# One order for VectorE's work in every iteration of a fused four-convolution kernel

## The chip, the cores and the metric

The kernel runs on one core of one Trainium2 chip. The metric is the device time of one execution, in microseconds (us). Before the change three runs gave 503.2, 502.8 and 504.18 us, median 503.2. The profiled execution, from which every duration below comes, took 501.05 us, and its span in the profile is 499.2 us.

Five engines matter: TensorE (PE in the profile; PEld is its weight load), VectorE (DVE), ScalarE (ACT), GpSimd (POOL) and SyncE (SP), which issues the transfers. Each works through its own queue in order[...].

## The reference

The input is `x` of 128 samples x 64 channels x 1024 positions and a style vector of 128 for each sample. Four convolution layers follow one another, and `x` is added to the result:

```python
def _layer(x, style, w, b, mw, mb, typ):
    s = style @ mw.T + mb
    weight = SCALE * w * s[:, None, :, None]
    demod = lax.rsqrt(jnp.sum(weight * weight, axis=(2, 3)) + EPS)
    weight = weight * demod[:, :, None, None]
    ...
    # same: conv of 3 taps; upsample: transposed conv by 2, then blur (1,3,3,1)
    # downsample: blur, then conv by 2
for i, typ in enumerate(('same', 'upsample', 'same', 'downsample')):
    out = _layer(out, style, weights[i], biases[i], mod_w[i], mod_b[i], typ)
return x + out
```

Everything in the chain is linear in `x` once a sample's style is known. The kernel therefore multiplies the four weight stacks of a sample into one kernel of nine taps (the chain), and convolves `x` once with it. The three positions at either end of a row, where the padding of the single layers matters, are computed apart (the "ends").

## The kernel before, in words

**Tiling.** Two samples make a pair; their 2 x 64 channels fill the 128 partitions. There are 64 pairs, `p` = 0 to 63. A matmul uses a 64 x 64 quarter of the array[...]. The main loop has 32 iterations, `q`, each with two pairs, `p` = 2q and p + 1. In its first half it finishes pair p, in its second pair p + 1.

**The convolution of one pair.** A row of `x` is split into three planes of 344 positions, and the nine taps into three groups of three; a short convolution identity then needs five products for each group of taps in place of nine. VectorE and GpSimd prepare five inputs, held in a tile `T`:

- G (`pre1`, L489 and L494): two VectorE operations on `X`. The load of a later pair's first plane is issued after it.
- T12 (`pre1`, L500 and L501): GpSimd makes two of the five inputs from G.
- T3 (`pre2a`, L512): VectorE, from `X`; the load of the later pair's other planes is issued after it.
- T04 (`pre2b`, L522): VectorE makes the last two from G.

TensorE does the products: `convA12` and `convA3` (products 1, 2 and 3) into a PSUM tile `psA`, and `convB` (products 0 and 4) into the bank pair `Y`. Between them lie sums:

- `m1`: ScalarE copies product 1 from PSUM (L567).
- `seed1`: VectorE makes u, v and y1 from `psA` and m1 (three operations, L573).
- `seed2`: VectorE writes two sums into `Y` (two operations, L573), onto which `convB` then accumulates. There is one `Y` for nearly all pairs, so `seed2` of a pair waits until ScalarE has read the outputs of the pair before out of it, and `convB` waits for `seed2`.
- `output` (L630): ScalarE scales and adds the constant, from `Y` and y1; `store` sends the result.

**The chain.** Two or three iterations ahead, TensorE multiplies the weights: `stage1`, `stage2`, `stage3` (L352, L383, L420), with ScalarE's scaled copies (`scale3`, L330) between them. `combine` (L450 to L463) is VectorE's last step: six groups of operations, written as H, that make the weights of products 1 to 3.

**Extras.** A table `EXTRA` hangs small pieces of work on halves of iterations, nearly all of it VectorE's: the second and third part of the modulation (iterations 1 to 7) and the ends (iterations 6 to 25). `(q, 0)` comes at the end of VectorE's work in the first half, `(q, 1)` in the second. `SLOTS` puts TensorE's small matmuls for these into the middle of `convB(p + 1)`.

**Order.** The schedule is manual: each engine runs its instructions in the order in which the program's lines emit them. TensorE's order in an iteration, with c = q + 2 and s = q + 3, is stage2(c), convB(p), stage3(c, 0), convA12(p + 2), stage3(c, 1), convA3(p + 2), convB(p + 1), stage1(s), convA12(p + 3), convA3(p + 3). The order of VectorE's work in an iteration before, for most q:

- first half: T3 and T04 of p + 3, G of p + 4, seed1 and seed2 of p + 1, EXTRA (q, 0);
- second half: T3 and T04 of p + 4, G of p + 5, seed1 and seed2 of p + 2, combine(c), EXTRA (q, 1).

Iterations 0, 1, 2 and 30 have orders of their own. Iteration 0 also holds the inverse, a Newton step and the table tA for the samples 16 to 31 (`var_inverse`, `var_newton`, `table_A` of `PART[1]`), ahead of T3(3).

**Start.** Before the first real matmuls, `zeros_to_y` multiplies zeros into `Y`; `blur_matmul` (L306) then builds the matrix `E` from the blur weights, and stage1(0), stage2(0) and so on fill the chain.

**End.** Pairs 60 and 62 use a bank pair of the chain's pool (`ps_w`, two tiles of one bank each), pair 61 uses `Y`, and pair 63 uses a tile of two banks from the pool of `psA`, which four matmuls of zeros touch first. A tile of two banks counts as one object when accesses are ordered.

Of the kernel before, what the change touches and what calls it, by code (L numbers as in the profile page):

```python
# [54 lines left out]
C = 64  # L55
# [8 lines left out]
def kernel(  # L64
# [99 lines left out]
    def zeros_to_y(sets, n, p=0):  # L164


        for i in range(sets):
            rows = HALF[i % 2]
            for cols in HALF:
                nc.tensor.matmul(  # L170
                    y_bank(p, i % 2)[cols, :n], Z[rows, :C], Z[rows, :n], start=True, stop=True
                )
# [51 lines left out]
    def var_inverse(bs, ls=slice(0, NL)):  # L224
        nc_v.reciprocal(dm[:, ls, bs], nw[:, ls, bs])
# [9 lines left out]
    def first_inverse(bs):  # L235

        nc_v.reciprocal(d2, nw[:, 2, bs])
        newton(var[:, 2, bs], d2, n2)
# [51 lines left out]
    def blur_matmul(ps):  # L290


        n = len(BLUR2)
        plan = [[], []]
        for b in range(n):
            for r, (lo, hi) in enumerate(((0, 5), (5, NT))):
                i, j = max(lo, b), min(hi, b + K)
                if i < j:
                    plan[r].append((b, i, j, lo))
        for k in range(max(map(len, plan))):  # L300
            for r, rows in enumerate(HALF):
                if k >= len(plan[r]):
                    continue
                b, i, j, lo = plan[r][k]
                for cols in HALF:
                    nc.tensor.matmul(  # L306
                        ps[r][cols, C * (i - lo) : C * (j - lo)],
                        idn[rows],
                        w1s[rows, min(b, n - 1 - b), i - b : j - b],
                        start=(k == 0),  # L310
                        stop=(k == len(plan[r]) - 1),
                        skip_group_check=True,
                    )
# [210 lines left out]
    def pre2(p):  # L524
        pre2a(p)
        pre2b(p)
# [25 lines left out]
    def convA12(p):  # L552
        if p >= NP:
            return
        ps = ps_conv.tile([P, 2, 512], F32, tag="u", name=f"psA{p}")
        m = [ps[:, :, i * NB : (i + 1) * NB] for i in range(3)]
        product(p, 1, [m[0][:, s] for s in range(2)])
        product(p, 2, [m[1][:, s] for s in range(2)])
        part[p] = m
# [37 lines left out]
    def seed(p):  # L597
        seed1(p)
        seed2(p)
# [22 lines left out]
    def output(p, s, eng=nc_a, parts=((0, 2), (2, 3))):  # L622

        b = 2 * p + s
        d3, add = dm[:, 3, b : b + 1], oc[:, b : b + 1]
        for i, j in parts:
            dst = os[p][:, s, i * NB : j * NB]
            src = y1s[p][:, s] if i == 2 else y_bank(p, s)[:, i * NB : j * NB]
            if eng is nc_a:
                nc_a.activation(dst, src, AF.Identity, bias=add, scale=d3)  # L630
            else:
                eng.tensor_scalar(dst, src, d3, add, op0=ALU.mult, op1=ALU.add)

    def store(p, s, at=slice(0, 3 * NB)):
        nc.sync.dma_start(out[p, :, s, at], os[p][:, s, at])
# [254 lines left out]
    LATER = slice(PART[0].stop, B)  # L890
    n_later = NL * (B - PART[0].stop)
    L2, L01, L3 = slice(2, 3), slice(0, 2), slice(3, 4)
    zeros_to_y(2, 256)
    zeros_to_y(2, 512)
    nc_v.tensor_scalar_mul(mbs, mb, SCALE)
    mod_matmul(PART[0], pm[0][0])

    nc_a.activation(wsq[T, L2], wio[T, L2], AF.Square)
    blur_scale((0, 1))
    zeros_to_y(2, 256)  # L900
    mod_scale(PART[0], pm[0][0])
    mod_square(PART[0])
    q2_sum(L2)
# [3 lines left out]
    nc_v.tensor_mul(wsq[T, L01], wio[T, L01], wio[T, L01])  # L907
    var_root(PART[0], pm[0][1], L2)
    blur_scale((2, 3))
    zeros_to_y(2, 192)  # L910
    nc_a.activation(wsq[T, L3], wio[T, L3], AF.Square)
    psB = [Y[:, r] for r in range(2)]
    blur_matmul(psB)
    first_inverse(PART[0])
    table_A(PART[0], d2)
    scale3(0, BOTH)
# [144 lines left out]
    for q in range(NQ):  # L1061
        p = 2 * q
        c, s = q + 2, q + 3
        if q == 1:
            nc.sync.dma_start(Xe, x_ends)
        if q == 5:
            zeros()
        if c < NQ:
            stage2(c)
        convB(p)  # L1070
        output(p, 0)

        if c < NQ:
            stage3(c, 0)
        output(p, 1, nc_a if q < NQ - 1 else nc_v)
        if q == NQ - 1:
            store(p, 0)
            store(p, 1)

            convB(p + 1)  # L1080
            for i in (2, 0, 1):
                for r, eng in enumerate(BOTH):
                    output(p + 1, r, eng, ((i, i + 1),))
                    if i != 2:
                        store(p + 1, r, slice(0, NB) if i == 0 else slice(NB, HO))
            break
        convA12(p + 2)
        if q:
            if q < 3:

                (seed2 if q == 1 else seed)(p + 1)
            if q < NQ - 2:
                pre2(p + 3)
            store(p, 0)
            pre1(p + 4)
            store(p, 1)
            if q > 2:
                seed(p + 1)
            if q == NQ - 2:
                pre2(p + 3)  # L1100
        else:
            store(p, 0)
            store(p, 1)
            seed2(p + 1)
            var_inverse(PART[1])
            var_newton(PART[1])
            table_A(PART[1], dm[:, 2, PART[1]])
            for of in (table_C, vector_c0, table_3, vector_Da):
                of(PART[1])
            pre2(p + 3)  # L1110
            pre1(p + 4)
        EXTRA.get((q, 0), lambda: None)()
        if c < NQ:
            stage3(c, 1)
        convA3(p + 2)
        if q == NQ - 2:
            convA12(p + 3)
        side = SLOTS.get(q)
        convB(p + 1, (lambda: slot(*side)) if side else None)
        output(p + 1, 0)  # L1120
        if q == NQ - 2:
            seed(p + 2)
            convA3(p + 3)

            Y2[p + 3] = unit(ps_conv, "Y3")
            zeros_to_y(2, 2 * NB, p + 3)
        output(p + 1, 1, nc_a if q < NQ - 2 else nc_v)
        if q == NQ - 2:
            seed_last(p + 3)
        if c == NQ - 1:  # L1130

            banks = unit(ps_w, "Y2")
            Y2[p + 2] = Y2[p + 4] = banks
            zeros_to_y(2, 2 * NB, p + 2)
        if q:
            pre2(p + 4)
            store(p + 1, 0)
            pre1(p + 5)
            store(p + 1, 1)
        if q < NQ - 2:  # L1140
            seed(p + 2)
        if s < NQ:
            stage1(s)
        if s + 1 < NQ:
            scale3(s + 1)
        if c < NQ:
                combine(c)
        if q == 0:
            store(p + 1, 0)
            store(p + 1, 1)  # L1150
            pre2(p + 4)
        EXTRA.get((q, 1), lambda: None)()
        if q < NQ - 2:
            convA12(p + 3)
            convA3(p + 3)
        if q == 0:
            seed1(p + 3)
            pre1(p + 5)


# [64 lines left out]
```

## Time and profile before

| | |
|---|---|
| median of the runs | 503.2 us |
| profiled execution | 501.05 us |
| its span | 499.2 us |
| ScalarE busy | 322.5 us (65%) |
| GpSimd busy | 133.7 us (27%) |
| transfers | 70.90 MB, 142 GB/s |

How the pieces cost, mean duration of one instruction: G 889 and 519 ns, T12 929 and 946 ns (GpSimd), T3 508 ns, T04 890 ns, u 503 ns, v 499 ns, y1 511 ns, one instruction of seed2 518 ns, the operations of H 550 to 566 ns with two of 278 ns between. Consecutive operations of VectorE overlap by some 0.08 us, so the time from one start to the next is a little less. A line of a timeline gives start, duration, engine, line, operation, output and inputs, shapes and count, and in brackets the idle time before it with what ended it.

### The profile page before, as it was taken

To read this page: it belongs to the slowest core of one execution; us is meant where nothing else is said; L and a number is where in the kernel's file an instruction comes from. 1 tells how busy PE (TensorE), PEld (TensorE's weight loads), DVE (VectorE), ACT (ScalarE), POOL (GpSimd) and SP (SyncE) were. 2 spreads that over 40 slices of the span, in tenths; PEclk is the share of its full clock that TensorE was granted. 3 is DMA by queue.
4 is the path that set the end of the run, shared out by engine and by line. 5 is a ranking of instruction groups with operands and counts; after the bars stand their busy time and mean duration, and the time that the engine had idled before them with its cause. 6 is when DMAs were issued, how large, how long until landed. Compare 5 with 4: busy or idle time off the path is not lost.

```text
span 499.2 us, 28320 instructions
## 1 busy us (share of the span) xinstructions
PE 487.2 (98%) x12616; PEld 474.9 (95%) x12616; DVE 444.0 (89%) x937; ACT 322.5 (65%) x788; POOL 133.7 (27%) x195
## 2 busy tenths in 40 slices
PE   7999999899999999999999999999999999999994
PEld 5899989899999999999999999999999999999994
DVE  4989999999999979987979998879999889888895
ACT  4546757567666667667667667657667666766643
POOL 2234315345222212212222122212212212221210
PEclk8999999999999999999999999999999999999998
DMA  8125535454444445353445444435355435443123
GB/s 260 46 61 170 178 116 169 144 171 140 147 146 149 145 137 164 126 164 122 144 145 161 127 157 153 144 124 163 125 146 165 141 123 189 148 141 130 69 106 127
DMA packets 37449, 70.90 MB, mean 142 GB/s; under 512 B 4176, under 2 KB 28752, under 8 KB 37328
## 3 DMA queue, kind: packets, MB, share of 16 engines
q1 hardware_dynamic: 37248, 68.85, 43.0%
q8 instruction: 99, 1.62, 1.4%
q10 hardware_dynamic: 80, 0.25, 0.1%
q14 instruction: 22, 0.18, 0.1%
HBM read 35.46 MB, written 33.62 MB: 138 GB/s over the span
## 4 chain that ended last, share of the span: by engine, by line
PE 85%; DVE 11%; issue 1%; ACT 1%; DMA 1%; SPq 0%; DVEq 0%
PE psA L540 29%; PE Y L540 19%; PE psR L383 15%; PE psW L420 13%; PE psS L352 6%; PE psE L780 2%; DVE T L522 2%; DVE G L489 2%; DVE Y L573 2%; DMA par_oi<-in_params_oi 1%; DVE G L494 1%; DVE u L573 1%; DVE T L512 1%; DVE v L573 1%; DVE H L458 0%
## 5 line engine op out<-in xcount | busy, mean ns | idle before, releaser
L540 PE MATMUL psA<-T,H 64*64 64x170 f32 x4608 | 207.9, 304 | 0.5 <-ACT R L330 0.3
L540 PEld LDWEIGHTS psA<-T,H 64*64 64x64 f32 x4608 | 190.8, 133 | 1.4 <-issue 0.8
L540 PE MATMUL Y<-T,Wf 64*64 64x170 f32 x3072 | 141.9, 304 | 3.1 <-DVE Y L573 2.8
L500 POOL TENSOR_TENSOR T<-G 128x342 f32<-128x342 f32 x62 | 57.6, 929 | 318.5 <-DVE G L494 189.7
L540 PEld LDWEIGHTS Y<-T,Wf 64*64 64x64 f32 x3072 | 128.8, 133 | 5.7 <-issue 2.3
L630 ACT ACTIVATE o<-Y,oc,dm 128x340 f32<-128x340 f32 (+1 forms) x126 | 79.8, 634 | 60.1 <-PE Y L540 59.4
L420 PE MATMUL psW<-R,par_oi 64*64 64x256 f32 (+3 forms) x1536 | 100.2, 349 | 0.0
L573 DVE SCALAR_TENSOR_TENSOR Y<-psA,u 128x340 f32<-128x340 f32 (+1 forms) x134 | 66.7, 502 | 35.2 <-ACT o L630 32.9
L383 PE MATMUL psR<-S,E 64*64 64x192 f32 (+1 forms) x2304 | 93.9, 299 | 0.4 <-ACT S L330 0.4
L330 ACT ACTIVATE Wf<-psW,t 128x256 f32<-128x256 f32 (+1 forms) x252 | 75.3, 381 | 23.3 <-PE psW L420 23.1
L420 PEld LDWEIGHTS psW<-R,par_oi 64*64 64x64 f32 x1536 | 86.2, 133 | 3.1
L383 PEld LDWEIGHTS psR<-S,E 64*64 64x64 f32 x2304 | 86.9, 133 | 0.6 <-ACT S L330 0.5
L330 ACT ACTIVATE R<-psR,tC 128x448 f32<-128x448 f32 x63 | 36.5, 630 | 56.0 <-PE psR L383 56.0
L630 ACT ACTIVATE o<-y,oc,dm 128x170 f32<-128x170 f32 x125 | 65.8, 526 | 0.4 <-DVE y L573 0.4
L501 POOL TENSOR_TENSOR T<-G 128x342 f32<-128x342 f32 x62 | 58.6, 946 | 0.0
L522 DVE TENSOR_TENSOR T<-G 128x684 f32<-128x684 f32 x64 | 57.0, 890 | 0.0
L489 DVE SCALAR_TENSOR_TENSOR G<-X 128x688 f32<-128x688 f32 x64 | 56.9, 889 | 0.0
L352 PE MATMUL psS<-wd,par_oi 64*64 64x192 f32 x768 | 46.1, 329 | 0.0
L352 PEld LDWEIGHTS psS<-wd,par_oi 64*64 64x64 f32 x768 | 38.4, 136 | 0.5 <-ACT raw L648 0.3
L567 ACT ACTIVATE m<-psA 128x340 f32<-128x340 f32 x64 | 29.2, 456 | 10.1 <-PE psA L540 4.9
L573 DVE SCALAR_TENSOR_TENSOR y<-psA,v 128x340 f32<-128x340 f32 x64 | 32.7, 511 | 2.2
L494 DVE SCALAR_TENSOR_TENSOR G<-X 128x342 f32<-128x342 f32 x64 | 33.2, 519 | 0.0
(132 smaller groups left out, 384.7 us busy)
## 6 DMA issues: line engine op xcount, KB each, us to landing
out<-o SPq DMA_DIRECT2D x126, 255.0 KB, 2.8
X<-in_x SPq DMA_DIRECT2D x60, 344.0 KB, 3.1
X<-in_x SPq DMA_DIRECT2D x60, 172.0 KB, 3.2
X<-in_x SPq DMA_DIRECT2D x4, 516.0 KB, 6.5
Xe<-in_x_ends SPq DMA_DIRECT2D x1, 512.0 KB, 3.6
par_oi<-in_params_oi SPq DMA_DIRECT2D x2, 208.0 KB, 4.8
out<-o SPq DMA_DIRECT2D x2, 170.0 KB, 2.5
par_io<-in_params_io ACTq DMA_DIRECT2D x1, 240.0 KB, 3.8
```

Of the source, the lines that this page charges most:

```text
L330: nc_a.activation(dst, src, AF.Copy, scale=f)
L352: nc.tensor.matmul(ps[r][cols, k * C : (k + K) * C], woi[rows, 2, k, :], src[rows, :], start=(k == 0), stop=(k == K - 1), skip_group_check ...
L383: nc.tensor.matmul(ps[r][cols, lo * C : (lo + m) * C], E[rows, e + 2, :], src[rows, a, :], start=(n == 0), stop=(n == 8), skip_group_check ...
L420: nc.tensor.matmul(ps[r][cols, (lo - t_lo) * C : (hi - t_lo) * C], woi[rows, 0, k, :], rt[c][rows, lo - k : hi - k, :], start=(k == order[0]),
L489: nc_v.scalar_tensor_tensor(g[:, PL:], X[:, : 2 * PL], 0.5, X[:, PL:], op0=ALU.mult, op1=ALU.subtract)
L494: nc_v.scalar_tensor_tensor(plane(g, 2), plane(X, 3), 0.5, plane(X, 2), op0=ALU.mult, op1=ALU.subtract)
L500: eng.tensor_add(t[:, 2, :NJ], plane(g, 2), plane(g, 1))
L501: eng.tensor_sub(t[:, 3, :NJ], plane(g, 2), plane(g, 1))
L522: nc_v.tensor_sub(t[:, 0:2, :NJ], both(a, PL), both(b, 1))
L540: nc.tensor.matmul(ps[s][cols], w, Ts[p][rows, SLOT[m], j : j + NB], start=(g == 0 and m not in (0, 4)), stop=(g == 2), skip_group_check=True,
L573: nc_v.scalar_tensor_tensor(out, x, f, y, op0=ALU.mult, op1=ALU.add)
L630: nc_a.activation(dst, src, AF.Identity, bias=add, scale=d3)
```

## The change

The two halves of all iterations get one order of VectorE's work: G; the sums from PSUM (seed1, seed2); H; then T3 and T04. In the first half: G(p + 4), seed1(p + 1), seed2(p + 1), T3 and T04 of p + 3, EXTRA. In the second half: G(p + 5), seed1(p + 2), combine(c), seed2(p + 2), T3 and T04 of p + 4, EXTRA. seed1(3) and G(5) of iteration 0 follow this too. The work on `PART[1]` goes from the first half of iteration 0 to the end of its second half, and scale3(4) therefore from iteration 0 to iteration 1, on ScalarE. Stores stand after G and after seed2, and the loads tied to G and T3 move with them.

At the end pairs 61 and 63 use the two bank tiles of the chain's pool, pairs 60 and 62 use `Y`, and the tile `Y3` and its zeros go. The last pair's outputs are written as one piece of 170 columns (y1) and one of 340, in place of three of 170.

At the start the zeros are cut differently, with four matmuls of zeros behind the blur matmuls, and one of the two lists in `blur_matmul` is reversed.

```diff
+        plan[1].reverse()
...
-    zeros_to_y(2, 256)
-    zeros_to_y(2, 512)
+    zeros_to_y(4, 256)
+    zeros_to_y(2, 128)
...
-    zeros_to_y(2, 256)
+    zeros_to_y(4, 192)
...
-    zeros_to_y(2, 192)
     nc_a.activation(wsq[T, L3], wio[T, L3], AF.Square)
     psB = [Y[:, r] for r in range(2)]
     blur_matmul(psB)
+
+    for rows, ps in zip(HALF, pm[1]):
+        for cols in HALF:
+            nc.tensor.matmul(ps[cols, :192], Z[rows, :C], Z[rows, :192], start=True, stop=True)
...
         output(p, 1, nc_a if q < NQ - 1 else nc_v)
+        if q == 1:
+            scale3(c + 1)
...
-            for i in (2, 0, 1):
+            for i, j in ((2, 3), (0, 2)):
                 for r, eng in enumerate(BOTH):
-                    output(p + 1, r, eng, ((i, i + 1),))
-                    if i != 2:
-                        store(p + 1, r, slice(0, NB) if i == 0 else slice(NB, HO))
+                    output(p + 1, r, eng, ((i, j),))
+                    store(p + 1, r, slice(i * NB, j * NB))
             break
         convA12(p + 2)
+
+        pre1(p + 4)
+        store(p, 0)
         if q:
-            if q < 3:
-
-                (seed2 if q == 1 else seed)(p + 1)
-            if q < NQ - 2:
-                pre2(p + 3)
-            store(p, 0)
-            pre1(p + 4)
-            store(p, 1)
-            if q > 2:
-                seed(p + 1)
-            if q == NQ - 2:
-                pre2(p + 3)
-        else:
-            store(p, 0)
-            store(p, 1)
-            seed2(p + 1)
-            var_inverse(PART[1])
-            var_newton(PART[1])
-            table_A(PART[1], dm[:, 2, PART[1]])
-            for of in (table_C, vector_c0, table_3, vector_Da):
-                of(PART[1])
-            pre2(p + 3)
-            pre1(p + 4)
+            seed1(p + 1)
+        seed2(p + 1)
+        store(p, 1)
+        pre2(p + 3)
         EXTRA.get((q, 0), lambda: None)()
...
-
-            Y2[p + 3] = unit(ps_conv, "Y3")
-            zeros_to_y(2, 2 * NB, p + 3)
...
-            Y2[p + 2] = Y2[p + 4] = banks
-            zeros_to_y(2, 2 * NB, p + 2)
-        if q:
-            pre2(p + 4)
+            Y2[p + 3] = Y2[p + 5] = banks
+            zeros_to_y(2, 2 * NB, p + 3)
+        if q < NQ - 2:
+            pre1(p + 5)
             store(p + 1, 0)
-            pre1(p + 5)
-            store(p + 1, 1)
-        if q < NQ - 2:
-            seed(p + 2)
+            seed1(p + 2)
+        else:
+            store(p + 1, 0)
         if s < NQ:
             stage1(s)
-        if s + 1 < NQ:
+
+        if q and s + 1 < NQ:
             scale3(s + 1)
         if c < NQ:
-                combine(c)
+            combine(c)
+        store(p + 1, 1)
+        if q < NQ - 2:
+            seed2(p + 2)
+        pre2(p + 4)
         if q == 0:
-            store(p + 1, 0)
-            store(p + 1, 1)
-            pre2(p + 4)
+            var_inverse(PART[1])
+            var_newton(PART[1])
+            table_A(PART[1], dm[:, 2, PART[1]])
+            for of in (table_C, vector_c0, table_3, vector_Da):
+                of(PART[1])
         EXTRA.get((q, 1), lambda: None)()
         if q < NQ - 2:
             convA12(p + 3)
             convA3(p + 3)
-        if q == 0:
-            seed1(p + 3)
-            pre1(p + 5)
```

## The prediction

> **What bounds the kernel now.** I read the page's busy shares first, then the list of waits, then the timelines of VectorE, TensorE, ScalarE and GpSimd over one iteration of the loop, and last the first 120 us and the last 10 us.
>
> ```profile
> PE 487.2 (98%) x12616; PEld 474.9 (95%) x12616; DVE 444.0 (89%) x937; ACT 322.5 (65%) x788; POOL 133.7 (27%) x195
> ```
>
> ```profile
> DVE Y L573 <- ACT o L630: 32.9, 34, 3.1
> ```
>
> TensorE is the bound: by the table of stretches it is busy without a gap from 150 to 475 us. An iteration (two pairs) takes it 14.40 us: the first convB of two neighbouring iterations starts at 351.22 and 365.61. So nothing on VectorE can make these iterations shorter; a new order there can only close the few gaps of the start (the idle before matmuls of convB: 0.53 us at 65.25, 1.72 at 89.30, 0.36 at 119.05) and of the end, or open gaps. The 32.9 us in which VectorE waits for ScalarE's output is therefore cover and not cost. The question is how late each VectorE result comes for the matmul that needs it.
>
> ```profile
> 351.22 0.30 PE L540 MATMUL Y<-T,Wf 64*64 64x170 f32 x1
> ...
> 365.61 0.30 PE L540 MATMUL Y<-T,Wf 64*64 64x170 f32 x1
> ```
>
> ```profile
> 355.60 0.65 ACT L630 ACTIVATE o<-Y,oc,dm 128x340 f32<-128x340 f32 x1
> ```
>
> ```profile
> 356.30 1.07 DVE L573 SCALAR_TENSOR_TENSOR Y<-psA,u 128x340 f32<-128x340 f32 x2
> 357.27 0.75 DVE L853 TENSOR_TENSOR Ue<-Ve 128x576 f32<-128x576 f32 x1
> 357.94 0.51 DVE L512 TENSOR_TENSOR T<-X 128x342 f32<-128x342 f32 x1
> 358.36 0.87 DVE L522 TENSOR_TENSOR T<-G 128x684 f32<-128x684 f32 x1
> 359.14 0.87 DVE L489 SCALAR_TENSOR_TENSOR G<-X 128x688 f32<-128x688 f32 x1
> 359.93 0.51 DVE L494 SCALAR_TENSOR_TENSOR G<-X 128x342 f32<-128x342 f32 x1
> ...
> 361.74 1.07 DVE L573 SCALAR_TENSOR_TENSOR Y<-psA,u 128x340 f32<-128x340 f32 x2
> 362.71 0.55 DVE L458 SCALAR_TENSOR_TENSOR H<-Wf 128x384 f32<-128x384 f32 x1
> ...
> 365.57 0.69 DVE L853 TENSOR_TENSOR Ve<-Ue 128x512 f32<-128x512 f32 x1
> ```
>
> The reader is to see two deadlines. Write S for the start of convB(p). seed2(p+1), at 356.30, can't start before ScalarE has read the bank (355.60 + 0.65 = 356.25), which is S + 5.07; call it A. seed2(p+2), at 361.74, ends at 362.81, while its matmul comes at 365.61: 2.8 us to spare, because combine (H, 2.86 us from 362.71 to 365.57) comes after it.
>
> Two smaller facts carry numbers below. The first matmul of convB waits for both instructions of seed2, not for the first alone: here they end at 64.13 + 1.06 = 65.19 and the matmul starts 0.06 later.
>
> ```profile
> 64.13 1.06 DVE L573 SCALAR_TENSOR_TENSOR Y<-psA,u 128x340 f32<-128x340 f32 x2
> ```
>
> ```profile
> 65.25 1.96 PE L540 MATMUL Y<-T,Wf 64*64 64x170 f32 x48 [0.53 <-DVE Y L573]
> ```
>
> And H, behind a GpSimd operation, takes 1.12 us in place of 0.55; the next operation starts 1.04 us after it, not 0.47, so 0.57 us was lost.
>
> ```profile
> 80.07 0.94 POOL L501 TENSOR_TENSOR T<-G 128x342 f32<-128x342 f32 x1
> ```
>
> ```profile
> 80.30 1.12 DVE L458 SCALAR_TENSOR_TENSOR H<-Wf 128x384 f32<-128x384 f32 x1
> 81.34 0.47 DVE L450 SCALAR_TENSOR_TENSOR Wf<-par_oi,t,Wf 128x64 f32<-128x64 f32 x2
> ```
>
> [...] G, T3, T04 and H (two SBUF inputs) are stretched beside GpSimd's T12 (T04 1.59 for 0.86 us at 56.17), while u, v, y1 and seed2 (one input in PSUM) keep 0.5 us. [...] The trace has 0.50 from 8 to 11 us.
>
> **The change part by part.** Of every operation the durations are those of before; only order and the two bank tiles change.
>
> *Second half of an iteration.* Before: T3 and T04 of p+4, G of p+5, seed1 and seed2 of p+2, combine. After: G, seed1, combine, seed2, then T3 and T04. From A the new queue is: seed2(p+1), T3 and T04 of p+3, the extra work E of this half iteration, G of p+5, seed1(p+2), combine, seed2(p+2). From the rows above: 356.30 to 361.74 less the extra 0.67 (357.27 to 357.94) is 4.77; combine 2.86; seed2 1.07; matmul 0.06. That is A + 8.76. To it comes a port wait: T12(p+5) starts 0.16 after G ends and lasts 1.80 (355.16 to 356.96 for one iteration of GpSimd), so it ends some 2.47 us after the second G starts; H is issued 1.81 us after that G, 0.66 before T12's end. At 80.30 the same overlap of 0.71 cost 0.57, so 0.52 here (bounds 0 and 0.66). S to S becomes 5.07 + 8.76 + 0.52 + E = 14.35 + E, against TensorE's 14.40. Without extras it just fits (0.05 to spare). With an extra, TensorE waits E - 0.05, and everything after shifts, as ScalarE's output hangs on convB.
>
> *The extras* of first halves, as spans from their first start to the next operation on VectorE's timeline: iteration 8 0.67, 10 1.05, 11 0.65, 15 and 16 1.35 each, 20 1.33, 21 0.67, 22 0.60, 23 0.53, 25 1.27: 9.47, less 10 x 0.05 = 9.0 us. Iteration 9's (0.61) is hidden, since the ends' matmuls lengthen that convB by 2.2 us. Extras of second halves stand behind seed2(p+2), with 5.07 - 3.6 = 1.5 us before the next A: hidden, except 0.3 of iteration 3's 1.76, which A's own slack takes.
>
> *Iterations 0 to 7.* G(4) moves ahead of seed2(1) (before: 40.30). [...] seed2(1) starts near 42.4 and convB(1) goes from 41.66 to 43.5. T3 and T04 of 3 then meet T12(4): done near 46.2; G(5), seed1(2), the port wait, combine and seed2(2) end at 53.2. convB(2) goes from 49.45 to 53.3. The inverse, Newton step and tA (2.0 us) move from before T3(3) to behind T04(4), so VectorE's sum of work is the same: convB(4) goes from 65.25 to 68.6, convB(6) from 80.48 to 83.8. There before loses time of its own (gaps above; spans between convA12 of 15.85, 15.43, 16.71 against 14.5 plus small matmuls), which after doesn't repeat in the same places: convB(8) 97.44 to 98.9. But iterations 3, 4, 6 and 7 have first-half extras of 0.66, 2.29, 1.36 and 0.60: convB(10) 112.09 to 115.6, convB(14) 141.80 to 145.9, convB(16) 156.37 to 160.9. Sum +4.5 (bounds +1 and +7[...]). scale3(4) on ACT (0.80) sits in iteration 1 behind output(2,1), under that lateness: nothing.
>
> *Start.* The zeros have 4864 columns before and after. Four of 192 now stand between blur and stage1, where TensorE has no gap (7.57 to 11.4): +0.2. If the clock no longer halves, up to -1.7 (3.4 us at 0.50); zeros between 5.8 and 6.4 go, so I take no gain. The reversed blur plan has the same matmuls, gated by par_oi at 7.57: nothing.
>
> *End.* Pair 63's banks become two tiles, so its last outputs needn't take turns:
>
> ```profile
> 494.05 0.45 DVE L632 TENSOR_SCALAR o<-Y,dm,oc 128x170 f32<-128x170 f32 x1 [0.56 <-ACT o L630]
> 494.54 0.49 ACT L630 ACTIVATE o<-Y,oc,dm 128x170 f32<-128x170 f32 x1 [0.52 <-DVE o L632]
> 495.07 0.46 DVE L632 TENSOR_SCALAR o<-Y,dm,oc 128x170 f32<-128x170 f32 x1 [0.56 <-ACT o L630]
> ```
>
> Both engines write 340 columns side by side from 493.5 to 494.2 in place of 495.53; the two stores still follow each other (0.35): -1.0. Zeros for Y3 (0.79) go, but convB(63) waits for the seed at 491.45 anyway. Stores and loads change places on SP; X is needed over 14 us after its load is issued: nothing.
>
> Sum: 4.5 + 9.0 + 0.2 - 1.0 = +12.7. The profiled execution took 501.05 (span 499.2), so 513.8; the runs' median, 503.2, lies 2.15 above it, so I forecast 515.9.
>
> **Rivals.**
> *No port wait at H.* T12 might be out of the way. Then each such iteration has 0.57 to spare: of the extras' 9.5 us 3.8 stays, the start loses some 2.5, and the end gives 0.8 net of the zeros: +5.5, 508.7. Against it: the identical pair of operations at 80.30.
> *Faster.* If convB's first product needed only the first seed2 instruction (0.5 us earlier) and H didn't wait, 1.1 us would be free in every iteration and nearly all extras hidden; G ahead of the sums would fill VectorE's waits, and before's own losses of iterations 1 to 6 (4.5 us) and 1.0 at the end would go, while 0.9 us of extras stayed (15, 16, 20 and 25): 498.6. It decides at E below 1.1. For it: VectorE is full from 50 to 100 us, partly with port waits that the new order avoids. Against it: 65.25, and the two other waits of TensorE on seed2, at 89.30 and 491.50, which start 0.14 and 0.05 us after the last seed instruction.
> *Not seen at all.* The losses and gains of the start cancel and the extras mostly hide: 503.
>
> **Numbers.** Main case 0.62 (own range 511 to 519), no port wait 0.15, faster 0.17, no change 0.06. A measurement can tell about 0.3% (1.5 us) from no change. Faster 0.17, same 0.06, slower 0.77. The range 504.5 to 519 holds the two slower cases: its low end is extras with all slack, its high end 0.1 more per iteration and +7 at the start.
>
> **What would show it.** Right: TensorE's idle before convB of even pairs, released by Y of VectorE, in iterations 8, 10, 11, 15, 16, 20 to 23 and 25, each about the extra's length; H near 1.1 us; 14.4 us in the others; outputs of pair 63 side by side. Wrong: no idle there, or seed2(p+2) ending over 1 us before its matmul.

## The result, and the profile after

In one session the changed kernel took 520.65 us (median of 6 runs, 518.83 to 522.52) where the kernel before took 502.76 us (6 runs, 501.28 to 504.18). The ratio is 1.0353 with a 95% interval of 1.0321 to 1.0385. The profiled execution took 520.9 us with a span of 519.1 us. The ratios below are of fast runs, so an execution of a1 that took 730.43 us at a mean granted clock of 0.659, where its others took 500 to 504, is left out of its ratio.

First the page's busy shares of the changed kernel, then three lines of its list of waits (engine, output and line, what it waited for, then us in total, times, longest), and last the line of the kernel before that belongs to the third.

```profile
PE 494.0 (95%) x12624; PEld 462.4 (89%) x12624; DVE 463.8 (89%) x934; ACT 321.4 (62%) x787; POOL 136.7 (26%) x195
```

```profile
DVE Y L574 <- ACT o L631: 29.1, 26, 2.9
PEld Y L541 <- DVE Y L574: 20.1, 21, 3.1
PE Y L541 <- DVE Y L574: 17.1, 18, 2.9
```

```profile
PE Y L540 <- DVE Y L573: 2.8, 3, 1.7
```

VectorE's share is 89% before and after, so the share tells nothing. The wait of TensorE does: before, it waited 2.8 us in 3 places for the seeds in `Y`; now it waits 17.1 us in 18 places, and the growth of the span is 19.9 us.

The second halves show the chain. This is the timeline of the changed kernel from iteration 27 to iteration 28, without extras, VectorE first, then GpSimd, then TensorE's two convB with what lies between left out.

```profile
460.94 1.07 DVE L574 SCALAR_TENSOR_TENSOR Y<-psA,u 128x340 f32<-128x340 f32 x2 [1.18 <-ACT o L631]
461.92 0.51 DVE L513 TENSOR_TENSOR T<-X 128x342 f32<-128x342 f32 x1
462.34 0.87 DVE L523 TENSOR_TENSOR T<-G 128x684 f32<-128x684 f32 x1
463.30 0.88 DVE L490 SCALAR_TENSOR_TENSOR G<-X 128x688 f32<-128x688 f32 x1
...
465.90 1.08 DVE L459 SCALAR_TENSOR_TENSOR H<-Wf 128x384 f32<-128x384 f32 x1
466.90 0.47 DVE L451 SCALAR_TENSOR_TENSOR Wf<-par_oi,t,Wf 128x64 f32<-128x64 f32 x2
...
469.29 1.07 DVE L574 SCALAR_TENSOR_TENSOR Y<-psA,u 128x340 f32<-128x340 f32 x2
```

```profile
464.77 0.92 POOL L501 TENSOR_TENSOR T<-G 128x342 f32<-128x342 f32 x1 [4.42 <-DVE G L495]
465.64 0.93 POOL L502 TENSOR_TENSOR T<-G 128x342 f32<-128x342 f32 x1
```

```profile
455.84 1.96 PE L541 MATMUL Y<-T,Wf 64*64 64x170 f32 x48
...
470.41 0.81 PE L541 MATMUL Y<-T,Wf 64*64 64x170 f32 x16
```

From S = 455.84 to the next S = 470.41 are 14.57 us, where TensorE's own work is 14.40. The last seed2 ends at 470.36, 0.05 before its matmul; before, it ended 2.8 us ahead. H takes 1.08 us in place of 0.55 and costs 0.53 from start to start, beside T12, which ends at 466.57; this delay shows as a longer instruction and not as a wait between two. It is what the prediction and the expectations call the port wait; over the 32 iterations this operation takes 0.95 us in the mean, against 0.57 before (one of 1.12 at 80.30, the others 0.55 to 0.56), and the traces give its length, not its cause. One thing was not in the prediction: G starts 0.96 us after T04 (462.34 to 463.30), where before it was 0.78 (358.36 to 359.14).

TensorE's timeline of the changed kernel, its waits at the end of iterations 15, 16 and 29:

```profile
286.82 1.96 PE L541 MATMUL Y<-T,Wf 64*64 64x170 f32 x48 [1.03 <-DVE Y L574]
302.58 1.96 PE L541 MATMUL Y<-T,Wf 64*64 64x170 f32 x48 [1.12 <-DVE Y L574]
...
499.64 1.70 PE L541 MATMUL Y<-T,Wf 64*64 64x170 f32 x20 [2.92 <-DVE Y L574]
```

Waiting is not all that TensorE loses. The granted clock, the share of full speed that the profile gives for TensorE, is 0.50 from 116.66 to 120.07 us and again from 498.95 to 502.37, each time at or just behind the end of one of its two longest waits (2.76 us until 115.55, 2.92 until 499.64). Two stretches of the changed kernel show the first; each line gives the stretch, its length, the busy time and count of PE, PEld, DVE, ACT and POOL, the granted clock, and the transfers.

```profile
113.25:116.66 3.41, 1.11 (x32) 1.11 (x36) 3.34 (x7) 0.72 (x2) 2.62 (x15) 1.00 0.01 2
116.66:120.07 3.41, 3.41 (x44) 2.44 (x40) 2.68 (x6) 1.05 (x2) 1.77 (x3) 0.50 0.58 155
```

At half clock the 48 matmuls of convB(60) take 3.27 us, where convB takes 1.96 at full clock.

Where the time went is read by laying the first matmul of each pair's convB beside its place in the kernel before, both counted from convB(0). The sum of the terms is the difference of the spans.

| stretch | predicted | profiled executions |
|---|---|---|
| start, to convB(0) | +0.2 | +0.35 |
| iterations 0 to 7, to pair 16 | +4.5 | +6.30 |
| iterations 8 to 28, to pair 58 | +9.0 | +10.58 |
| end | -1.0 | +2.66 (+3.25 to pair 63, -0.59 behind it) |
| sum | +12.7 | +19.9 |

These are single executions, and the first row is less than starts differ from execution to execution: the changed kernel reaches convB(0) at 35.41 us, six kernels below with the same start at 34.76 to 36.93.

### The profile page after: what moved, and what is told of

It is laid out like the page before. It is cut to its first block, busy times and chain, and to the rows that moved or that the text cites. A ratio compares the mean times of both kernels' runs of the same rounds, so it can differ in the third digit from the quotient of the medians.

```text
span 519.1 us, 28314 instructions
## 1 busy us (share of the span) xinstructions
PE 494.0 (95%) x12624; PEld 462.4 (89%) x12624; DVE 463.8 (89%) x934; ACT 321.4 (62%) x787; POOL 136.7 (26%) x195
## 3 DMA queue, kind: packets, MB, share of 16 engines
q8 instruction: 99, 1.62, 1.4%
## 5 line engine op out<-in xcount | busy, mean ns | idle before, releaser
L541 PE MATMUL psA<-T,H 64*64 64x170 f32 x4608 | 188.0, 304 | 0.3 <-ACT R L331 0.3
L541 PEld LDWEIGHTS psA<-T,H 64*64 64x64 f32 x4608 | 171.2, 133 | 1.3 <-ACT R L331 0.5
L541 PE MATMUL Y<-T,Wf 64*64 64x170 f32 x3072 | 129.8, 309 | 17.2 <-DVE Y L574 17.1
L541 PEld LDWEIGHTS Y<-T,Wf 64*64 64x64 f32 x3072 | 113.0, 134 | 27.0 <-DVE Y L574 20.1
L631 ACT ACTIVATE o<-Y,oc,dm 128x340 f32<-128x340 f32 x125 | 79.5, 636 | 76.2 <-PE Y L541 74.1
L421 PE MATMUL psW<-R,par_oi 64*64 64x256 f32 (+3 forms) x1536 | 87.9, 353 | 0.0
L421 PEld LDWEIGHTS psW<-R,par_oi 64*64 64x64 f32 x1536 | 64.0, 134 | 13.5 <-issue 0.9
L353 PE MATMUL psS<-wd,par_oi 64*64 64x192 f32 x768 | 40.0, 324 | 0.0
L574 DVE SCALAR_TENSOR_TENSOR u<-psA,m 128x340 f32<-128x340 f32 x64 | 32.4, 506 | 3.3 <-ACT m L568 3.3
L353 PEld LDWEIGHTS psS<-wd,par_oi 64*64 64x64 f32 x768 | 32.4, 134 | 1.0 <-ACT raw L649 0.3
```

What stands on the lines that cost most here:

```text
L353: nc.tensor.matmul(ps[r][cols, k * C : (k + K) * C], woi[rows, 2, k, :], src[rows, :], start=(k == 0), stop=(k == K - 1), skip_group_check ...
L421: nc.tensor.matmul(ps[r][cols, (lo - t_lo) * C : (hi - t_lo) * C], woi[rows, 0, k, :], rt[c][rows, lo - k : hi - k, :], start=(k == order[0]),
L541: nc.tensor.matmul(ps[s][cols], w, Ts[p][rows, SLOT[m], j : j + NB], start=(g == 0 and m not in (0, 4)), stop=(g == 2), skip_group_check=True,
L574: nc_v.scalar_tensor_tensor(out, x, f, y, op0=ALU.mult, op1=ALU.add)
```

## The experiments

The theory on trial: seed2(p + 2) behind combine closes a chain through ScalarE's outputs, seed2, T3 and T04, extras, G, the sums, H with its delay beside T12, and seed2 again, and its length, not TensorE's work, now sets each iteration. The chief rival: VectorE simply has too much to do in a row, whatever the order of seed2 and combine. In the diffs the new order is that of the kernel named.

### a1: seed2 ahead of combine

```diff
+        if q < NQ - 2:
+            seed2(p + 2)
         if c < NQ:
             combine(c)
         store(p + 1, 1)
-        if q < NQ - 2:
-            seed2(p + 2)
```

> The changed kernel with one move back: in every second half seed2(p+2) stands before combine again, as before the change. Theory (the chain from ScalarE's last read of the bank to seed2(p+2) is what ends late): the chain loses combine and the port wait (2.86 + 0.52 us), so TensorE's idle before convB of even pairs vanishes in iterations 8 to 25 (9.5 us) and before pair 60 (2.9 us); what stays is at most the start, so 501 to 506 us. Rival (VectorE's sum of work, or its port waits, bound the iterations, and the order within one doesn't matter): 518 to 522, with the idle moved elsewhere.

Measured: 501.2 us, ratio to the kernel before 1.0008 (0.9995 to 1.0021). With two steps exchanged the whole loss is gone; the same VectorE work is done, so the rival falls for the loop. The timeline of a1 in iteration 28, VectorE and then TensorE:

```profile
462.81 1.08 DVE L574 SCALAR_TENSOR_TENSOR Y<-psA,u 128x340 f32<-128x340 f32 x2 [0.20 <-ACT o L631]
463.79 0.55 DVE L459 SCALAR_TENSOR_TENSOR H<-Wf 128x384 f32<-128x384 f32 x1
```

```profile
466.70 0.30 PE L541 MATMUL Y<-T,Wf 64*64 64x170 f32 x1
```

seed2 ends at 463.89, 2.8 us ahead of its matmul, and H, now behind T12, takes 0.55. Every iteration from 8 to 28 is back, within 0.05 us, at the length it has before. Three things stay. Pair 1 comes 1.07 us later than before (G(4) ahead of seed2(1), as e1 below shows). Pair 3 comes 2.90 later, which e1 does not cure; by pair 7 a1 is 0.67 earlier than before. And pair 61 loses 1.8 us to a wait taken up below.

### a2: extras in the time in which VectorE waits

```diff
         if q:
             seed1(p + 1)
+        EXTRA.get((q, 0), lambda: None)()
         seed2(p + 1)
         store(p + 1, 1)
         pre2(p + 3)
-        EXTRA.get((q, 0), lambda: None)()
```

> The changed kernel with the extras of the first halves put between seed1(p+1) and seed2(p+1), where VectorE waits about 1.2 us for ScalarE. Theory: extras up to about 1 us leave the chain, the long ones (1.35 us) leave 0.2 to 0.7 us each; TensorE's idle of iterations 8 to 25 falls from about 9.5 to 3 us, that of iterations 3 to 7 by 2 to 3 us; the rest stays: 509 to 513 us, and iterations without extras stay at 14.52 to 14.58 us. Rival (sum of VectorE's work): no change, 518 to 522.

Measured: 517.3 us, ratio 1.0328 (1.0302 to 1.0354): missed. The extras do leave the chain in part: iteration 20 falls from 15.69 to 14.60 us, but 21 only from 15.06 to 14.98 and 16 from 15.76 to 15.35. The timeline of a2, GpSimd and VectorE in iteration 16, tells why:

```profile
288.99 0.92 POOL L502 TENSOR_TENSOR T<-G 128x342 f32<-128x342 f32 x1
```

```profile
289.26 1.27 DVE L827 SCALAR_TENSOR_TENSOR Ue<-b1s,Ue 128x576 f32<-128x576 f32 x1
290.56 0.56 DVE L832 SCALAR_TENSOR_TENSOR Ue<-b1s,Ue 64x64 f32<-64x64 f32 x2
291.15 1.07 DVE L574 SCALAR_TENSOR_TENSOR Y<-psA,u 128x340 f32<-128x340 f32 x2
```

The wait before seed2 is just the time in which T12 runs. The extra meets it at 289.26 and takes 1.27 us, where it takes 0.75 in the changed kernel, and seed2 starts without any wait left, late. The expectation had counted the empty time and not the delay beside T12. Part of the miss lies elsewhere: iteration 4 became longer (18.82 us in place of 17.40), and after its wait of 2.51 us TensorE has half clock from 107.72 to 111.14.

### a3: T12 of second halves on VectorE, out of H's way

```diff
+        t12 = None
         if q < NQ - 2:
-            pre1(p + 5)
+            if p + 5 < NP:
+                g01, g2, t12 = pre1(p + 5, None)
+                g01()
+                g2()
...
         pre2(p + 4)
+        if t12:
+            t12(nc_v)
```

> The changed kernel with T12 of the second halves made by VectorE behind T04(p+4), so that no GpSimd operation stands beside H. VectorE gets 0.85 us more work in each iteration, behind seed2(p+2). Theory with the port wait as priced (0.52 us of the chain): H's first operation falls from 1.07 to 0.55 us, iterations without extras go to 14.39, those with extras lose 0.5 us of their idle each (14 of them, with those of iterations 3 to 7), and 0.5 before pair 60: 6 to 9 us less, 512 to 515. If the port wait is no part of the chain: no change or slower, 520 to 527, since the work grows by 27 us in all.

Measured: 512.93 us, ratio 1.0238 (1.0203 to 1.0273), as expected. VectorE has 0.85 us more to do in an iteration and the kernel is faster than the changed one by 1%: H's delay beside T12 lies in the chain, the sum of the work does not. The timeline of a3, VectorE from iteration 27 to 28:

```profile
457.97 0.55 DVE L459 SCALAR_TENSOR_TENSOR H<-Wf 128x384 f32<-128x384 f32 x1
...
463.00 0.51 DVE L501 TENSOR_TENSOR T<-G 128x342 f32<-128x342 f32 x1
463.43 0.51 DVE L502 TENSOR_TENSOR T<-G 128x342 f32<-128x342 f32 x1
463.85 0.87 DVE L490 SCALAR_TENSOR_TENSOR G<-X 128x688 f32<-128x688 f32 x1
...
467.46 1.08 DVE L574 SCALAR_TENSOR_TENSOR Y<-psA,u 128x340 f32<-128x340 f32 x2 [0.93 <-ACT o L631]
```

H is at 0.55 and VectorE waits 0.93 us for ScalarE afterwards: T12 fits into slack. Iterations without extras last 14.39 to 14.44 us, those with extras about 0.5 less than in the changed kernel.

### a4: seed2 ahead of combine in iteration 29 alone

```diff
+        if q == NQ - 3:
+            seed2(p + 2)
         if c < NQ:
             combine(c)
         store(p + 1, 1)
-        if q < NQ - 2:
+        if q < NQ - 3:
             seed2(p + 2)
```

> The changed kernel with seed2 before combine in iteration 29 alone (for pair 60). Theory: TensorE has only some 11.5 us of work in that iteration since the chain's stages have ended, and the 2.92 us of idle before convB(60) are the same chain: they go, 517 to 518.5 us. Rival (the new bank tiles of pairs 61 and 63 lengthen the end by themselves): at most 0.5 us less.

Measured: 517.48 us, ratio 1.0339 (1.0321 to 1.0356). By the traces pair 60 follows pair 58 after 11.54 us in place of 14.65 (11.49 in the kernel before), and the span falls from 519.1 to 516.4, by 2.7 us. The end is thus one more link of the same chain. a4 has no half clock at the end, and then waits 1.80 us for `psA`, a wait that the changed kernel does not have: of the 3.11 us won at pair 60, 2.43 are left at pair 63.

### b1: a third tile for G

```diff
-    gpool = ctx.enter_context(tc.tile_pool(name="gpool", bufs=2))
+    gpool = ctx.enter_context(tc.tile_pool(name="gpool", bufs=3))
```

> The changed kernel with a third buffer for the tiles G. In the changed order the first operation of G(p+5) overwrites the tile that T04(p+3), just ahead of it, reads, and it starts 0.96 us after T04 where 0.78 was usual. Theory: with a third buffer these 0.17 us leave the chain in second halves without an extra, so iterations 13, 17, 18 and 26 to 28 fall from 14.52 to 14.58 to 14.39 us; with an extra in between nothing changes: 1 to 1.5 us less than the changed kernel, 517 to 520. Rival[...]: no change of the 0.96.

Measured: 518.6 us, ratio 1.0335 (1.0312 to 1.0357); its interval overlaps that of the changed kernel, so the trace must tell. The timeline of b1, VectorE:

```profile
461.37 0.87 DVE L523 TENSOR_TENSOR T<-G 128x684 f32<-128x684 f32 x1
462.15 0.87 DVE L490 SCALAR_TENSOR_TENSOR G<-X 128x688 f32<-128x688 f32 x1
```

G again starts 0.78 us after T04. With two tiles, G of p + 5 overwrites the G of p + 3 that T04 just ahead of it reads, and the next instruction starts only when T04 is done. The program orders the two itself: T04 raises a semaphore of VectorE in 44 of its 64 cases in the changed kernel, in 1 in b1 and in the kernel before, and VectorE waits for this semaphore 318 times in the changed kernel, 275 times in b1. Iterations 13, 17, 18 and 26 to 28, which have no extra, fall from 14.52 to 14.71 us to 14.39 to 14.48; those with an extra, which stands between T04 and G, stay as they are. b2 below agrees: there T04 and G use different tiles, and the same six iterations last 14.39 to 14.48 us. Pair 58 comes 2.8 us earlier than in the changed kernel, 1.9 of it already at pair 16. Of that, 1.7 has nothing to do with the tile: it is the half clock of the changed kernel from 116.66 to 120.07 us, which b1's execution doesn't have. Both wait 2.76 us before convB(10). The changed kernel's timeline of the weight loads shows stops there:

```profile
118.50 0.26 PEld L421 LDWEIGHTS psW<-R,par_oi 64*64 64x64 f32 x4 [0.27 <-issue]
119.03 0.26 PEld L421 LDWEIGHTS psW<-R,par_oi 64*64 64x64 f32 x4 [0.27 <-issue]
```

"issue" means that the engine waited for nothing that the profile shows as an event; the clock is shown in another view. Why b1 keeps its clock is taken up in the last section.

### b2: the kernel before, with seed2 behind combine

```diff
         if q < NQ - 2:
-            seed(p + 2)
+            seed1(p + 2)
...
                 combine(c)
+        if q < NQ - 2:
+            seed2(p + 2)
```

> The kernel before with one part of the change alone: in second halves seed2(p+2) goes behind combine. Theory: the same chain, 14.35 us plus the extra, since G, seed1, H with its wait for T12 and seed2 follow A in the same way: about 9 us in iterations 8 to 25, about 3 before pair 60, 1 to 4 in iterations 3 to 7: 12 to 16 us above before, about the whole loss of the change. Rival (several parts of the change make the loss together): under 8 us above before.

Measured: 530.54 us, ratio 1.0593 (1.0556 to 1.063), twice the loss expected. The expected part is there: from pair 16 to 58 it loses 9.67 us (expected: about 9), and the iterations with extras are as long as in the changed kernel within 0.02 us. The unexpected part is the start: pair 16 comes 15.03 us late, against 6.30 in the changed kernel. TensorE's timeline of b2 has the waits:

```profile
52.26 1.96 PE L540 MATMUL Y<-T,Wf 64*64 64x170 f32 x48 [1.86 <-DVE Y L573]
70.47 3.37 PE L540 MATMUL Y<-T,Wf 64*64 64x170 f32 x48 [3.48 <-DVE Y L573]
90.93 3.38 PE L540 MATMUL Y<-T,Wf 64*64 64x170 f32 x48 [3.64 <-DVE Y L573]
```

In the second and third line the same 48 matmuls take 3.37 and 3.38 us in place of 1.96, since b2 has half clock from 69.99, 90.47 and 124.60 us, each time for 3.41 us and at the end of a wait of 2.77 to 3.64. The changed kernel has one such stretch in these iterations. So the rest of the change (G and the sums first, T3 and T04 last, the work on `PART[1]` later) gives back 8.7 us of what its one bad step costs in the first iterations; by an estimate from 3.41 us at 0.50, up to 3.4 of these are two stretches at half clock that it avoids. Which of the three parts gives it was not separated.

### b3: the kernel before, with the end's tiles and outputs alone

```diff
-            for i in (2, 0, 1):
+            for i, j in ((2, 3), (0, 2)):
...
-            Y2[p + 3] = unit(ps_conv, "Y3")
-            zeros_to_y(2, 2 * NB, p + 3)
...
-            Y2[p + 2] = Y2[p + 4] = banks
+            Y2[p + 3] = Y2[p + 5] = banks
```

> The kernel before with the change's end alone: pairs 61 and 63 in the chain's two bank tiles, 60 and 62 in Y, the last outputs in two pieces. Theory: the last outputs run side by side on ScalarE and VectorE, 0.5 to 1.0 us less than before; pair 60 isn't late, as seed2(60) stands ahead of combine. Rival (the bank tiles lengthen the end): 1 to 3 us more.

Measured: 500.65 us, ratio 0.9978 (0.9959 to 0.9996), 1.1 us (0.2 to 2.1). Its profile puts 0.27 us behind pair 63 (7.47 us from there to the end in place of 7.74). Of its other 0.9 us nearly all lies where the edit can have no part: 0.51 before convB(0), and 0.34 by pair 7. So that the outputs alone give 1.1 us is not shown. In the changed kernel itself the two outputs do stand side by side:

```profile
513.95 0.63 ACT L631 ACTIVATE o<-Y,oc,dm 128x340 f32<-128x340 f32 x1 [0.37 <-PE Y L541]
514.11 0.63 DVE L633 TENSOR_SCALAR o<-Y,dm,oc 128x340 f32<-128x340 f32 x1
```

### Toward a faster version: e1, f1, f2 and f3

e1 is a1 with three repairs: seed2(1) ahead of G(4) in iteration 0, T04(62) behind the sums of pair 61, and the third G tile.

```diff
+        if q == 0:
+            seed2(p + 1)
         pre1(p + 4)
...
+        if q == NQ - 2:
+            seed_last(p + 1)
+            pre2b(p + 2)
...
-        pre2(p + 4)
+        pre2a(p + 4)
+        if q != NQ - 3:
+            pre2b(p + 4)
```

> The kernel of the first experiment (seed2 ahead of combine) with three repairs: seed2(1) ahead of G(4) in iteration 0, seed2(61) ahead of y1(61) and T04(62) (TensorE waited 1.8 us there for psA), a third G tile. Theory: 1.0 us less at the start, up to 1.7 at the end: 1.5 to 3 us under the kernel before, 497.5 to 499.5 where before gives 500.7. If the start is bound by VectorE's sum of work: 0 to 1.5 us under before.

Measured: 502.28 us, ratio 1.0006 (0.9992 to 1.0021): missed. Pair 1 wins its 1.07 us, but at pair 3 nothing is left of it: e1 is 3.01 us later than before there, a1 2.90, since TensorE now waits 2.65 us at once before convB(3). The first repair moved the lateness from iteration 0 into iteration 1. And then it costs more: pair 4 comes 3.37 us late, in a1 1.62, because e1 has half clock just behind this wait.

```profile
61.26:64.67 3.41, 3.41 (x56) 3.41 (x52) 2.90 (x6) 0.98 (x3) 0.77 (x1) 0.50 0.59 160
```

The 22 executions of e1 form two groups, 8 from 499.52 to 500.80 us and 14 from 501.94 to 503.27; the profiled one (503.26) is of the second. That the others of that group lose their clock at the same place is likely and not shown. The second repair works: from pair 58 to 63 e1 takes 24.22 us, a1 24.82.

The f kernels go the other way: from b3, with the order of a1 only in a range of iterations.

```diff
+        new = 3 <= q < NQ - 3
+        if new:
+            pre1(p + 4)
+            store(p, 0)
+            seed(p + 1)
+            store(p, 1)
+            pre2(p + 3)
-        if q:
+        elif q:
...
+        if new:
+            pre1(p + 5)
+            store(p + 1, 0)
-        if q:
+        elif q:
...
+        if new:
+            store(p + 1, 1)
+            pre2(p + 4)
```

This is f3. In f1 the range begins at 2, in f2 at 3, and in both it ends with 29.

> The kernel before with pair 63's outputs side by side (as in b3), and in iterations 2 to 28 alone the changed order of VectorE's work, with the second seed2 ahead of combine; iterations 0, 1, 29 and 30 keep the order of before. Theory: what was good in the change is the order G, sums, then T3 and T04 in iterations 2 to 7 (a1 went from +1.61 us against before at pair 4 to -0.67 at pair 7), what was bad is seed2(1) behind G(4) in iteration 0, seed2 behind combine everywhere, and the end. Then convB(7) comes 2.2 us earlier than in the kernel before, that stays to the end, and with 0.5 to 1.0 for the outputs the time is 497.5 to 499 us where the kernel before takes 501, ratio 0.993 to 0.997. Rival: a1 only caught up from a late start, TensorE's work sets pair 7 in any case: then as b3, ratio 0.998, convB(7) 54.2 us after convB(0).

> As f1, but the changed order begins in iteration 3 and iteration 2 is that of the kernel before. Theory: the 1.72 us that TensorE waits before convB(7) in the kernel before come from T3(9), G(10) and the port in iteration 3 itself, so most of the 2.2 us is gained here too: 498 to 499.5 us, ratio 0.994 to 0.998. Rival: it is iteration 2's order that sets it (T3 and T04 of 7 ahead of G): then convB(7) stays 54.2 us after convB(0) and the ratio is that of b3, 0.998.

> As f2, but iteration 29 too keeps the order of the kernel before; the changed order, with seed2 ahead of combine, runs in iterations 3 to 28 alone. In f2 pair 58 came 1.37 us earlier than in the kernel before and pair 63 0.2 us earlier only: T3 and T04 of pair 62, last in iteration 29, push the sums of pair 61 behind them (482.65 in place of 481.30), and TensorE waits 1.78 us for the bank that they read. Theory: with T3 and T04 of 62 first again in iteration 29, pairs 60 to 63 come 23.7 us after pair 58 as in b3, and f2's gain stays: 1.4 us at pair 58 and 0.5 to 1.0 at the outputs, so 498.7 to 499.8 us where the kernel before takes 501.2, ratio 0.995 to 0.997. Rival: the wait before convA of pair 62 comes from another stage of the end that the changed order of iteration 28 also delays: then pair 63 stays where f2 has it, ratio 0.999.

| | median us | ratio, interval | pair 7 against before | pair 58 | pair 63 |
|---|---|---|---|---|---|
| f1 | 500.72 | 0.9989, 0.9976 to 1.0003 | -0.36 | -0.48 | +0.66 |
| f2 | 501.18 | 0.9991, 0.998 to 1.0002 | -1.54 | -1.37 | -0.21 |
| f3 | 499.99 | 0.996, 0.9945 to 0.9975 | -0.75 | -0.58 | -0.65 |

f1 and f2 missed their forecasts. f1's profiled execution has a stop of TensorE of 1.52 us that ends at 67.74 and that no releaser explains (the last section takes it up), and what it would be without that can't be read. f2's gain at pair 7 is there, and is lost at the end. A delay beside T12 in iteration 3, the port of its expectation, does not show: in the kernel before T3(9) takes 0.51 us there, and G(10), at 85.49, 0.87 and 0.51, as elsewhere. VectorE's and TensorE's timelines of f2:

```profile
480.98 0.55 DVE L463 SCALAR_TENSOR_TENSOR H<-Wf,H 128x384 f32<-128x384 f32 x1
481.44 0.51 DVE L512 TENSOR_TENSOR T<-X 128x342 f32<-128x342 f32 x1
481.87 0.86 DVE L522 TENSOR_TENSOR T<-G 128x684 f32<-128x684 f32 x1
482.65 0.51 DVE L573 SCALAR_TENSOR_TENSOR u<-psA,m 128x340 f32<-128x340 f32 x1
```

```profile
485.24 1.99 PE L540 MATMUL psA<-T,H 64*64 64x170 f32 x48 [1.78 <-DVE Y L573]
```

T3 and T04 of pair 62 stand between H and the sums of pair 61, and TensorE waits for the `psA` that these sums read. The changed kernel and a1 have the same order there; a1 has the same wait. f3 takes the old order in iteration 29, the wait is gone (pair 61 follows pair 59 after 12.14 us in place of 13.34), and the kernel is 0.4% faster than the kernel before. That is what f3's forecast said, but not by the way that it said: pair 58 comes 0.58 us earlier, not 1.4. Of its median gain of 1.5 us b3 as a whole already has about 1.1; that f3 beats b3 is not shown, the intervals overlap. In convB(4) its profiled execution has a stop of the weight loads without a releaser of 0.69 us, where f2's, at the same place, is 0.36.

## Why the prediction was right or wrong

**Right.** The direction, and the mechanism with its place and price. a1 shows that seed2 behind combine is the whole loss of iterations 8 to 28. The formula 14.35 + E was met where it was to hold: iteration 8 15.07 us (15.02 by the formula), 10 15.42 (15.40), 15 15.70 (15.70), 20 15.69 (15.68), 25 15.62 (15.62). Iteration 9 is hidden as said. H's delay beside T12 is 0.53 us (taken: 0.52), and a3 shows that it lies in the chain. Why VectorE's operation is longer there was not shown; what the traces have is 1.08 us in place of 0.55 for H and 1.27 in place of 0.75 for a2's extra. The outputs side by side go with 0.59 us less behind pair 63 (0.27 in b3).

**Wrong: the end.** The step "End: ... -1.0" priced only the bank tiles and outputs. The chain was worked out as 14.35 + E against TensorE's 14.40, and that comparison was carried to all iterations, but in iteration 29 TensorE has no stage of the chain left to do and needs 11.49 us. There the chain is not 0.05 us too short but 3.2 us too long (14.65). Pair 60 comes 3.16 us late. The end cost +2.66 in place of -1.0, the biggest miss of the sum (3.7 us). a4's span is 2.7 us shorter, 2.4 of it by pair 63. What is left in a4, 0.8 us at pair 63, fits T3 and T04 of pair 62 ahead of pair 61's sums, which f3 against f2 shows to be worth 1.2 us there. In the changed kernel itself TensorE, late and at half clock, does not wait for these sums; what the half clock of its end costs alone was not separated.

**Wrong in size: "Without extras it just fits (0.05 to spare)".** Six iterations (13, 17, 18 and 26 to 28) last 14.52 to 14.71 us in place of 14.39, together 1.2 us of the 1.6 between 9.0 and 10.58. The missing term is the G tile that T04 still reads, 0.18 us wherever no extra stands between the two: b1, without it, wins 0.93 us from pair 16 to 58, all in these six. The iterations with extras lose 9.38 in place of 9.0.

**Wrong in size: iterations 0 to 7, 4.5 against 6.30.** The steps to pair 10 were near and on the high side (pair 4 +2.42 for +3.35, pair 8 +0.58 for +1.5, pair 10 +3.32 for +3.5). The excess comes between pairs 10 and 11, from the half clock at 116.66: iteration 5 takes 16.24 us, in b1, without it, 14.51, and b1 has +4.42 at pair 16. The step that failed is the price of a wait: the prediction weighed the clock for the start alone, and took a wait of TensorE at its own length. Here the wait of 2.76 us cost 1.7 us more. Two of the changed kernel's six executions, with a mean clock of 0.997 in place of the profiled 0.990, took 518.83 and 518.85 us.

**Slips that changed nothing.** S + 5.07 is the start of seed2(p+1), at 356.30; ScalarE ends at S + 5.03. The places of convB(8), (10), (14) and (16) before are 97.22, 111.88, 141.53 and 156.10, 0.2 to 0.3 us ahead of those given; only differences entered the sum. The terms of the rival without a delay of H give some +5.2 us, not +5.5.

**The offset.** 2.15 us were added for the distance of the runs' median from the profiled execution. The changed kernel's profiled 520.9 lies at its median, so this addition covered part of the miss by luck: the sum was 7.2 us short, the forecast 4.75.

**The start, by luck.** No gain was taken from the clock at the start, and the +0.35 is near the +0.2 taken. But the half clock there comes and goes from execution to execution, as the last section shows, and moves convB(0) by more than that.

**The rivals.** H without a delay beside T12: out, by the 1.08 us. Faster, from a first seed2 instruction that frees the matmul: out, since the waits end 0.05 us after the second. Nothing seen: out.

## What to carry to other kernels

A chain that just fits under the bound in the steady loop is to be compared with the bound again in each iteration where the bound is shorter, the last ones first. A long wait of TensorE is to be priced above its length: in the loops of these profiles 12 of the 13 waits of 2.3 us or more went with 3.41 us at half clock, up to 1.7 us more each, and none of the waits up to 2.08 us did. Behind a3's wait of 2.33 us, until 490.85, the 48 matmuls of convB take 3.51 us; behind a2's of 2.08 us, until 53.78, they take 1.96. Before an operation is put into an engine's empty time, look at what runs on the neighbour engine in that very time: here it was T12, beside which H took 1.08 us in place of 0.55 and a2's extra 1.27 in place of 0.75. And where a write is moved directly behind the read of the same buffer, on the same engine, and the program makes the write wait for the read, the overlap of the two instructions is lost (0.96 us from start to start in place of 0.78); here a third buffer gave it back.

## What was not expected of the hardware

Two instructions of one engine, the second of which overwrites what the first reads, start 0.96 us apart in place of 0.78 (T04 to G, with two and three G tiles): the second starts only when the first has ended (463.21 and 463.30 us in the changed kernel). As the program has it wait for the first, it is not shown that the chip would hold it back by itself.

Twelve waits of TensorE, of 2.3 to 3.64 us, went with half clock for 3.41 us each, and most of them are shorter than that stretch. In each trace all changes of the granted clock lie whole multiples of 3.413 us apart (in the changed kernel 105.81 us is 31 of them, 378.88 is 111; in the kernel before 484.69 is 142). Cut each of the 13 profiles at these places, from convB(0) to 3 us before the end: all 14 stretches in which TensorE was idle for 1.95 us or more are followed by one at half clock, and none of the others is, with up to 1.87 us of idle time (in the changed kernel 2.30, 2.24 and 1.95 us against at most 1.36, in the kernel before 2.45 against 1.72). So in these traces it matters where a wait falls. The 2.76 us before convB(10) put 2.30 us into one stretch of the changed kernel (113.25 to 116.66), and half clock follows; in b1 the same wait is shared by two, with 1.81 and 0.95 us, and the clock stays.

At the start the half clock is no matter of the kernel before alone. Its trace has a granted clock of 0.50 from 7.80 to 11.21 us. In the other twelve the first entry of the clock record is a change to full clock at 9.47 to 13.53 us; ahead of it there is none, and the view prints 1.00. The matmuls show that the clock was half there as well: b2's 24 matmuls of the first stage1, in a stretch that the view gives as 1.00, take 2.09 us, those of the kernel before 2.11; b3's, behind the change at 9.72, take 1.17. First b2, then b3:

```profile
10.08 2.09 PE L352 MATMUL psS<-wd,par_oi 64*64 64x192 f32 x24
```

```profile
9.81 1.17 PE L352 MATMUL psS<-wd,par_oi 64*64 64x192 f32 x24
```

b2 and b3 have the same start, so the cut of the zeros does not decide it. convB(0) of these two starts at 35.74 and 34.55 us.

Five profiles (before, b3, f1, f2 and f3) have stops of TensorE's weight loads without a releaser between 50 and 83 us, of 0.25 to 1.83 us, at full clock. They differ in length, but stand at only four places of TensorE's own order, at its 2242nd, 2754th, 3010th or 3779th record. A line of f1's weight loads, then one of its page's list of transfer queues (packets, MB, share of the engines' time):

```profile
67.74 0.33 PEld L540 LDWEIGHTS Y<-T,Wf 64*64 64x64 f32 x9 [1.83 <-issue]
```

```profile
q8 instruction: 99, 1.62, 1.4%
```

Each of these 13 stops ends 1.1 to 1.6 us after a packet of the queue that the page calls "instruction" (f1: the packet from 65.35 to 66.25, the stop until 67.74; the kernel before: packets until 59.80 and 79.86, stops of 0.53 and 0.29 us until 61.29 and 81.26). What TensorE waits for in these stops was not shown; no run tested it.
